# Regrouping the end of the attention layer and moving the load of x_out in a two-layer graph network

## The chip, the cores and the metric

The kernel runs on one core of one Trainium2 chip. The metric is the device time of one execution in microseconds, as the median of several runs.

## The reference, cut to what matters

There are 1250 nodes with 512 features and 40000 edges, sorted by destination. The first layer is graph attention with 8 heads, followed by a feed-forward network with Gelu; the second layer adds up messages along the same edges and runs a batch-normed two-layer network.

```python
# first layer, per edge (source s, destination d), 8 heads of 64 channels
e     = sum_c( leaky_relu(xl[s] + xr[d], 0.2) * att )
alpha = softmax of e over the edges of one destination
x     = x + sum over edges( alpha * xl[s] ) + bias
x     = x + gelu(layernorm(x) @ W1 + b1) @ W2 + b2
x     = layernorm(x_in + x)
# second layer
aggr  = sum over edges( relu(x[s] + edge_attr @ W_e + b_e) )
h     = (1 + eps) * x + aggr
h     = silu(bn(h @ V1 + c1)) @ V2 + c2
out   = layernorm(x + silu(bn(h)))
```

## The kernel before, in words

Nodes are sorted by their number of incoming edges and cut into ten blocks of 128 (one node per partition). Block b has KB[b] edge slots per node: 44, 40, 37, 35, 33, 32, 31, 29, 27, 25. "Row" below means one edge slot of one block: 128 rows of a table, gathered by one indirect DMA that GpSimd (POOL) issues. The first layer has 333 such gathers (tile xg, from the table xl_t), the second layer another 333 (tile xs, from the table xb_t).

**The first layer** (function `attention`) takes the blocks from 9 down to 0. A block is cut into groups of at most 20 rows, and a group into chunks of at most 5 rows (CN). Here G0 and G1 are the groups of block 1 in the kernel before, H0, H1 and H2 those of block 0 (20, 16 and 8 rows). For every chunk, `scores` gathers the rows and runs three long VectorE (DVE) instructions on them (two into z, one into S). After the last chunk of a group, `softmax` takes the running maximum, and ScalarE (ACT) takes the exponential into w. One group later, `weigh` multiplies the rows of each chunk by w: the first `na` rows on ACT, eight instructions a row, the others in one DVE instruction; then TensorE (PE) adds the rows up in PSUM (tile pacc, one buffer, two matmuls a row). Two groups later, `merge` adds pacc to the block's sum on DVE, at chunk 0 of that group. So at every chunk the program issues the scores of one group and the weighing of the group before it; in the last chunk of a group all that is left of that weighing is issued at once.

When a block is merged for the last time, `head_of` normalises it and transposes it (hT), and `body_of` runs its feed-forward network: 16 steps f, each with eight matmuls into pu, a Gelu on ACT into uT and two matmuls into py two steps later. The steps are fed into the other work by calls of `part()`, three to a chunk (the quota). `end_of` adds py, normalises again, and writes the block twice: a plain store to xo_t from the SP queue, and a scatter to xb_t from POOL. Chunks of rows lie in seven buffers (GB); a buffer comes free when PE has added its rows.

The instructions of `attention` on DVE, ACT, PE and POOL go through wrappers (V, A, T, G) that keep the order of the program on their engine. Instructions that are written with `nc.vector` or `nc.scalar`, as in `begin`, `features_of` and `second`, have no such order: the scheduler puts them where it finds room.

**The second layer** (function `second`) first loads all of xo_t into x_out by ten loads of 256 KB from the SP queue. Then it walks the edges in units of 8 (block 9 first): `turn` transposes the edge features on PE and copies them to eaT, `edges` gathers four rows at a time into xs (five buffers), PE computes the edge term pe, and DVE runs two instructions for every pair of rows (`tensor_add`, then a maximum and a sum into pd). `finish` needs x_out of its block after the block's last edge. Features of an edge span are gathered by `features_of`; a span that doesn't start at slot 0 first gets a small DVE instruction (wx, line 1428).

All instructions of the wrappers show line 1059 in the profile; they are told apart by their tiles.

Of the kernel before, what the change touches and what calls it, by code (L numbers as in the profile page):

```python
# [7 lines left out]
F32 = mybir.dt.float32  # L8
BF16 = mybir.dt.bfloat16
I32 = mybir.dt.int32  # L10
AF = mybir.ActivationFunctionType
# [5 lines left out]
P = 128  # L17
# [5 lines left out]
ED = 64  # L23
# [699 lines left out]
def gnn_kernel(ctx, tc, x, src, dst, edge_attr, ln1_g, ln1_b, Wl, Wr, att, gat_bias,  # L723
# [301 lines left out]
    def short_path():  # L1025
        with ExitStack() as sa:
            fast = sa.enter_context(tc.tile_pool(name="fast", bufs=1))
            fdram = sa.enter_context(tc.tile_pool(name="fdram", bufs=1, space=DRAM))
            xb_t = fdram.tile([N + 1, D], F32, name="xb_t")
            xo_t = fdram.tile([NP, D], F32, name="xo_t")  # L1030
            eps1 = row(eps, 1, "eps1", fast)
            nc.vector.tensor_scalar(eps1, eps1, 1.0, None, op0=OP.add)
            back = fast.tile([P, P], F32, name="back")
            nc.vector.tensor_scalar(back, jp, float(-V0), None, op0=OP.is_equal)
            lone = fast.tile([P, 1], F32, name="lone")
            nc.vector.tensor_scalar(lone, jp[:, 0:1], float(-VN), -0.1 * BIG, op0=OP.is_le, op1=OP.mult)
            s2 = sa.enter_context(ExitStack())
            early = {}
            with ExitStack() as s1:
                attention(s1, xb_t, xo_t, back, lone, lambda: begin(s2, early))  # L1040
            second(s2, early, xb_t, xo_t, eps1, back)

    def attention(s1, xb_t, xo_t, back, lone, follow):

# [121 lines left out]
        def body_of(b, y, hT):  # L1166

            py = aq.tile([P, D], F32, name="py", bufs=2)
            nf = FF // P
            uTs = []  # L1170
            for f in range(nf + 2):
                if f < nf:
                    pu = aq.tile([P, P], F32, name="pu", tag="pu", bufs=3)
                    for k in range(KD):
                        T.matmul(pu, w1[:, k, f * P:(f + 1) * P], hT[:, k, :], start=(k == 0), stop=(k == KD - 1))
                    uT = bp.tile([P, P], F32, name="uT", bufs=4)
                    A.activation(uT, pu, AF.Gelu, bias=cols[:, f:f + 1])
                    uTs.append(uT)
                if f == nf:
                    held["hT"] -= 1  # L1180
                if f >= 2:
                    T.matmul(py, uTs[f - 2], w2[:, f - 2, :], start=(f == 2), stop=(f == nf + 1))
                yield
            others.append(end_of(b, y, py))
# [90 lines left out]
        def weigh(g):  # L1275

            w, n = g["w"], g["n"]
            g["gd"] = gd = sp.tile([P, HEADS], F32, name="gd")
            V.tensor_reduce(gd, w[:, :n, :].rearrange("p n h -> p h n"), axis=AX.X, op=OP.add)
            g["pacc"] = aq.tile([P, D], F32, name="pacc")  # L1280
            for c, (c0, cn) in enumerate(g["cuts"]):
                na = (cn + c % 2) // 2
                xv = g["xg"][c][:, na:cn, :].rearrange("p n (h c) -> p n h c", c=CX)[:, :, :, 0:CH]
                V.tensor_mul(xv, xv, w[:, c0 + na:c0 + cn, :, None].to_broadcast([P, cn - na, HEADS, CH]))
                for j in range(c0, c0 + cn):
                    if j < c0 + na:
                        xv = row_of(g, j)
                        for h in range(HEADS):
                            A.activation(xv[:, h, :], xv[:, h, :], AF.Copy, scale=w[:, j, h:h + 1])
                    if g["quota"] > 0:  # L1290
                        g["quota"] -= 1
                        part()
                    add_up(g, j)
                yield
# [50 lines left out]
        over = {}  # L1345
        groups = []
        for b in ORDER:
            cuts = [(0, 20), (20, 16), (36, 8)] if b == 0 else parts(KB[b], GN)
            for k0, n in cuts:
                groups.append(dict(b=b, k0=k0, n=n, first=(k0 == 0), last=(k0 + n == KB[b]), cuts=parts(n, CN), xg=[]))  # L1350
        groups[0]["cuts"] = [(0, 2)] + [(2 + a, k) for a, k in parts(groups[0]["n"] - 2, CN)]
# [4 lines left out]
        for i, g in enumerate(groups):  # L1356
            if g["first"]:
                if i:
                    blk, ahead = ahead, None
                blk["m"] = low  # L1360
                if g["b"] == 0:
                    drain("acc", 1)
                    held["acc"] += 1
                    blk.update(over)
            g["blk"] = blk
            g["S"] = sp.tile([P, GN + 1, HEADS], F32, name="S")
            nc_ = len(g["cuts"])
            for c in range(nc_):
                scores(g, c)
                if c == nc_ - 1:  # L1370
                    softmax(g)
                if c == 0:
                    if g["first"] and g["b"] != ORDER[-1]:
                        ahead = normed_of(g["b"] - 1)
                    if g["last"]:
                        rows_of(blk)
                        if ahead:
                            others.append(xr_of(ahead))
                    if merging:
                        merge(merging)  # L1380
                    weighing = weigh(before) if before else None
                step_others()
                todo = 0
                if weighing:
                    todo = len(before["cuts"]) - c if c == nc_ - 1 else 1
                quota = 3
                for _ in range(todo):
                    before["quota"] = quota
                    next(weighing, 0)
                    quota = before["quota"]  # L1390
                for _ in range(quota):
                    part()
                step_lates()
            merging, before = before, g
# [7 lines left out]
        while going or done or ready or others:  # L1402
            step_others()
            part()
            step_lates()

    def begin(s2, early):

# [21 lines left out]
        gather(ea[:, :en * ED], edge_attr, wx)  # L1430
        return ea

    def second(s2, early, xb_t, xo_t, eps1, back):

        vp = s2.enter_context(tc.tile_pool(name="vp", bufs=1))
        v1, v2, we, ep = (early[k] for k in ("v1", "v2", "we", "ep"))
        x_out = vp.tile([P, NB, D], F32, name="x_out")
        for b in (NB - 1, *range(NB - 1)):
            nc.sync.dma_start(x_out[:, b, :], xo_t[b * P:(b + 1) * P, :])
        hT = vp.tile([P, KD, N], F32, name="hT5")  # L1440
        z1 = vp.tile([P, 2 * KD, N], F32, name="z1")
        st1 = vp.tile([P, 2 * KD, 3, 6], F32, name="st1")
# [18 lines left out]
        with ExitStack() as s3:  # L1461
# [2 lines left out]
            hq = s3.enter_context(tc.tile_pool(name="hq", bufs=1, space=PSUM))  # L1464
            pend = {u: ea for u, ea in zip(spans, early["features"])}

            def turn(b, e0, en, c0, cn):

                at = spans.index((b, e0, en))
                if c0 == 0:  # L1470
                    for u in spans[at:at + 2]:
                        if u not in pend:
                            pend[u] = features_of(ep, *u)
                ea = pend[b, e0, en]
                pt = hq.tile([P, KD, P], F32, name="pt5")
                eaT = ep.tile([P, KD, P], F32, name="eaT")
                for j in range(0, cn, 2):
                    wd = min(2, cn - j) * ED
                    nc.tensor.transpose(pt[:wd, j // 2, :], ea[:, (c0 + j) * ED:(c0 + j) * ED + wd], ident)
                full = cn // 2  # L1480
                if full:
                    nc.scalar.copy(eaT[:, :full, :], pt[:, :full, :])  # L1482
                if cn % 2:
                    nc.scalar.copy(eaT[:ED, full, :], pt[:ED, full, :])
                return eaT

            def edges(b, at0, cn, eaT, pd):
                for d0 in range(0, cn, 4):
                    dn = min(4, cn - d0)
                    xs = xp_.tile([P, 4, D], F32, name="xs")  # L1490
                    for j in range(dn):
                        at = at0 + d0 + j
# [1 line left out]
                    for j in range(0, dn, 2):  # L1494
# [4 lines left out]
                            kk = P if m == 2 else ED  # L1499
                            nc.tensor.matmul(pe[:, i, :], eaT[:kk, q, :], we[:kk, i, :], start=True, stop=True)  # L1500
                        xv = xs[:, j:j + m, :]
                        nc.vector.tensor_add(xv, xv, pe[:, :m, :])  # L1502
                        nc.vector.scalar_tensor_tensor(pd[:, :m, :], xv, 0.0, pd[:, :m, :], op0=OP.max, op1=OP.add)  # L1503
                    yield

            def finish(b, pd):
# [8 lines left out]

            units = [(b, e0, en, c0, min(8, en - c0)) for b, e0, en in spans for c0 in range(0, en, 8)]
            work, at = None, 0
            eaT = turn(*units[0])
            for n, (b, e0, en, c0, cn) in enumerate(units):
                if e0 == 0 and c0 == 0:  # L1520
                    pd = hq.tile([P, 2, D], F32, name="pd")
                    if b == 0:
                        nc.tensor.matmul(pd[:, 0, :], back, h9, start=True, stop=True)
                        nc.vector.memset(pd[:, 1, :], 0.0)
                    else:
                        nc.vector.memset(pd, 0.0)
                ahead = turn(*units[n + 1]) if n + 1 < len(units) else None
                for _ in edges(b, KO[b] + e0 + c0, cn, eaT, pd):
                    if work is not None and next(work, 0) == 0:
                        work = None  # L1530
# [128 lines left out]
```

## Time and profile before

| what | value |
|---|---|
| median of 3 runs | 1665.33 us (1662.75 to 1666.01) |
| profiled execution | 1664.86 us, span 1663.1 us |
| granted TensorE clock, mean | 0.906 |
| PE / DVE / ACT / POOL busy | 1295.3 / 1286.2 / 631.2 / 833.5 us |
| scores of block 1 begin | 754.24 us |
| last pacc matmul ends | 991.5 us |
| last scatter to xb_t issued | 1042.19 us |
| first gather of the second layer | 1048.28 us |
| last gather of the second layer | 1495.5 us |

Times are microseconds from the start of the span. In lines of the timeline the columns are start, duration, engine, line, operation, tiles and shape, count, and in brackets how long the engine was idle before and what it waited for. In the table of stretches the columns are the length, and for each engine the busy time and the number of instructions, then the granted clock, the busy share of the DMA engines and the rate.

### The profile page before, as it was taken

The page shows a single profiled execution, that of the slowest core. Times are in us where ns is not written, and L with a number is a line of the kernel's source. Part 1 is how long each engine was busy: PE and PEld are TensorE (multiplying, and loading weights), DVE is VectorE, ACT ScalarE, POOL GpSimd, SP SyncE. Part 2 cuts the span into 40 slices and gives each one's busy share as a digit, 9 for nine tenths or more (in the row PEclk, how much of TensorE's full clock was granted, in tenths as well). Part 3 has the DMA queues.
Part 4 walks back from the last instruction along what each step waited for, and adds up shares of the span by engine and source line. Part 5 has one row for each costly group of instructions (what it writes and reads, how often), then busy time and mean ns, then how long its engine had stood idle before and what let it go on. Part 6 is the DMA issues. An engine that isn't in the chain of part 4 may idle for free.

```text
span 1663.1 us, 14065 instructions
## 1 busy us (share of the span) xinstructions
PE 1295.3 (78%) x4281; PEld 660.7 (40%) x4281; DVE 1286.2 (77%) x1384; ACT 631.2 (38%) x1900; POOL 833.5 (50%) x762
## 2 busy tenths in 40 slices
PE   5752678888878886869697889587888898889891
PEld 5430225454444443525253446233333343334451
DVE  4918999898888889898999841598999689986123
ACT  0211456666556565657565663000000110001422
POOL 1058755444535465554646410677777757770002
PEclk9975779899989898979899899799989999999995
DMA  4526764343434343544444313777777757770001
GB/s 141 217 68 179 255 210 132 97 118 89 125 93 139 106 135 96 140 108 124 133 118 110 102 49 133 231 227 217 226 223 222 217 165 219 226 208 9 1 1 64
DMA packets 77857, 235.79 MB, mean 142 GB/s; under 512 B 14689, under 2 KB 15167, under 8 KB 77261
## 3 DMA queue, kind: packets, MB, share of 16 engines
q0 software_dynamic: 60160, 200.09, 41.7%
q1 hardware_dynamic: 16205, 32.12, 5.4%
q10 hardware_dynamic: 1408, 2.60, 0.4%
q8 instruction: 36, 0.59, 0.1%
q14 instruction: 48, 0.39, 0.1%
HBM read 216.71 MB, written 18.17 MB: 141 GB/s over the span
## 4 chain that ended last, share of the span: by engine, by line
PE 28%; DVE 16%; issue 16%; ACT 14%; DMA 10%; POOL 5%; SPq 0%; DVEq 0%; POOLq 0%; ACTq 0%
PE pacc L1059 12%; ACT xg L1059 9%; DMA xs<-xb_t,src_i 7%; DVE z L1059 5%; PE pu L1059 5%; PE py L1059 4%; POOL xs L746 3%; DVE pd L1503 3%; PE pe L1500 3%; DVE S L1059 2%; ACT L1059 2%; DMA xg<-xl_t,src_i 2%; PE pm L1059 2%; DVE xs L1502 2%; PE pz L1449 1%
## 5 line engine op out<-in xcount | busy, mean ns | idle before, releaser
L1059 POOL DMA_INDIRECT xg<-xl_t,src_i x333 | 425.6, 1278 | 335.2 <-issue 192.4
L1059 PE MATMUL pacc<-xg,ident 128*128 128x512 f32 x666 | 382.7, 698 | 186.1 <-ACT xg L1059 178.8
L746 POOL DMA_INDIRECT xs<-xb_t,src_i x333 | 317.3, 953 | 117.2 <-issue 78.6
L1500 PE MATMUL pe<-we,eaT 128*128 128x512 f32 x666 | 332.7, 632 | 49.2 <-DVE xs L1502 48.0
L1059 ACT ACTIVATE xg<-xg,w 128x64 f32<-128x64 f32 x1344 | 333.8, 338 | 0.0
L1059 PEld LDWEIGHTS pacc<-xg,ident 128*128 128x128 f32 x666 | 133.7, 216 | 393.7 <-ACT xg L1059 271.8
L1059 DVE TENSOR_TENSOR z<-xg,nxr 128x2600 f32<-128x2600 f32 (+2 forms) x75 | 192.0, 2559 | 67.1 <-DMA xg<-xl_t,src_i 40.4
L1502 DVE TENSOR_TENSOR xs<-xs,pe 128x1024 f32<-128x1024 f32 (+1 forms) x170 | 202.8, 1193 | 38.2 <-DMA xs<-xb_t,src_i 22.9
L1059 PEld LDWEIGHTS pu<-hT,w 128*128 128x128 f32 x1280 | 180.9, 204 | 84.7 <-issue 77.0
L1500 PEld LDWEIGHTS pe<-we,eaT 128*128 128x128 f32 x666 | 121.3, 199 | 225.5 <-DVE xs L1502 111.7
L1503 DVE SCALAR_TENSOR_TENSOR pd<-xs,pd 128x1024 f32<-128x1024 f32 (+1 forms) x170 | 204.4, 1202 | 1.5
L1059 DVE TENSOR_TENSOR z<-z,patt 128x2600 f32<-128x2600 f32 (+2 forms) x75 | 191.9, 2559 | 2.6
L1059 DVE TENSOR_REDUCE S<-z 128x40 f32<-128x2600 f32 (+2 forms) x75 | 191.8, 2558 | 2.6
L1059 PE MATMUL pu<-hT,w 128*128 128x128 f32 x1280 | 183.5, 290 | 4.1 <-ACT hT L1059 4.1
L1059 PE MATMUL py<-w,uT 128*128 128x512 f32 x320 | 169.8, 615 | 1.7 <-ACT uT L1059 1.7
L1059 ACT ACTIVATE uT<-pu,cols 128x128 f32<-128x128 f32 x160 | 58.2, 365 | 130.1 <-PE pu L1059 129.6
L1482 ACT COPY eaT<-pt 128x512 f32<-128x512 f32 (+3 forms) x46 | 24.7, 537 | 208.7 <-PE pe L1500 173.9
L1059 DVE TENSOR_TENSOR xg<-xg,w 128x1024 f32<-128x1024 f32 (+2 forms) x75 | 98.9, 1322 | 0.0
L738 POOL DMA_INDIRECT out_dram<-o,v_i x10 | 9.9, 990 | 146.3 <-DVE o L1620 143.6
L1059 ACT ACT_TABLE_LOAD x63 | 80.8, 1283 | 5.4 <-PE pu L1059 4.3
L1449 PE MATMUL pz<-hT,v 128*128 128x512 f32 (+1 forms) x192 | 72.3, 518 | 5.3 <-ACT z L1457 5.3
L1574 PE MATMUL pz<-z,v 128*128 128x512 f32 (+1 forms) x192 | 70.4, 528 | 5.2 <-ACT z L1565 5.2
(222 smaller groups left out, 914.3 us busy)
## 6 DMA issues: line engine op xcount, KB each, us to landing
w<-in_L_gnn_W_dram SPq DMA_DIRECT2D x8, 1024.0 KB
xg<-xl_t,src_i POOLq DMA_INDIRECT x333, 3.8
xs<-xb_t,src_i POOLq DMA_INDIRECT x333, 3.7
v<-in_L_gnn_W_dram SPq DMA_DIRECT2D x2, 2048.0 KB
xo_t<-xo SPq DMA_DIRECT2D x10, 256.0 KB
x_out<-xo_t SPq DMA_DIRECT2D x10, 256.0 KB
xl_t<-xo ACTq DMA_DIRECT2D x9, 260.0 KB
x_sb<-in_x_dram SPq DMA_DIRECT2D x1, 2304.0 KB
```

What stands on the lines that cost most here:

```text
L738: s = nc.gpsimd.indirect_dma_start(out=table, out_offset=bass.IndirectOffsetOnAxis(ap=idx, axis=0), in_=rows, in_offset=None, bounds_check ...
L746: return nc.gpsimd.indirect_dma_start(out=rows, out_offset=None, in_=table, in_offset=bass.IndirectOffsetOnAxis(ap=idx, axis=0))
L1059: ins = getattr(engine, name)(*args, **kw)
L1449: nc.tensor.matmul(pz[:, :nn], w[:, k, f * P:(f + 1) * P], src_t[:, k, n0:n0 + nn], start=(k == 0), stop=(k == nk - 1))
L1482: nc.scalar.copy(eaT[:, :full, :], pt[:, :full, :])
L1500: nc.tensor.matmul(pe[:, i, :], eaT[:kk, q, :], we[:kk, i, :], start=True, stop=True)
L1502: nc.vector.tensor_add(xv, xv, pe[:, :m, :])
L1503: nc.vector.scalar_tensor_tensor(pd[:, :m, :], xv, 0.0, pd[:, :m, :], op0=OP.max, op1=OP.add)
L1574: nc.tensor.matmul(pzs[i][:, :nn], v2[:, k, f * P:(f + 1) * P], z1[:, k, n0:n0 + nn], start=(k == 0), stop=(k == 2 * KD - 1))
```

## The change: what it does

1. Block 1 is cut into groups of 16, 14 and 10 rows instead of 20 and 20; block 0 into 10, 16, 10 and 8 rows instead of 20, 16 and 8. The projection of the next block (`xr_of`) starts at the second group of a block instead of the last.
2. In the very last group ACT weighs one row of each chunk instead of two.
3. In the body of block 0 an activation with Sqrt on a dummy column follows the last Gelu.
4. The first two copies to eaT and the first memset of pd in the second layer go through the wrappers A and V, and so stand behind the last instructions of the first layer on ACT and DVE.
5. The ten loads of x_out are issued in the first unit of edges, behind the `tensor_add` that ends its second step, and that unit's steps are 2, 4 and 2 rows instead of 4 and 4.

```diff
+                V, A = attention(s1, xb_t, xo_t, back, lone, lambda: begin(s2, early))
+            second(s2, early, xb_t, xo_t, eps1, back, V, A)
...
                 if f == nf:
                     held["hT"] -= 1
+                    if not b:
+                        A.activation(sp.tile([P, 1], F32, name="none_"), ln_eps, AF.Sqrt)
...
-                na = (cn + c % 2) // 2
+                na = 1 if g is groups[-1] else (cn + c % 2) // 2
...
-            cuts = [(0, 20), (20, 16), (36, 8)] if b == 0 else parts(KB[b], GN)
+            cuts = {0: [(0, 10), (10, 16), (26, 10), (36, 8)], 1: [(0, 16), (16, 14), (30, 10)]}.get(b, parts(KB[b], GN))
...
                     if g["last"]:
                         rows_of(blk)
-                        if ahead:
-                            others.append(xr_of(ahead))
+                    if ahead and i and groups[i - 1]["first"]:
+                        others.append(xr_of(ahead))
...
         x_out = vp.tile([P, NB, D], F32, name="x_out")
-        for b in (NB - 1, *range(NB - 1)):
-            nc.sync.dma_start(x_out[:, b, :], xo_t[b * P:(b + 1) * P, :])
...
-            def turn(b, e0, en, c0, cn):
+            def turn(b, e0, en, c0, cn, act=nc.scalar):
...
-                    nc.scalar.copy(eaT[:, :full, :], pt[:, :full, :])
+                    act.copy(eaT[:, :full, :], pt[:, :full, :])
...
-                for d0 in range(0, cn, 4):
-                    dn = min(4, cn - d0)
+                for d0, dn in [(0, 2), (2, 4), (6, 2)] if at0 == KO[NB - 1] else [
+                        (d, min(4, cn - d)) for d in range(0, cn, 4)]:
...
-                        nc.vector.tensor_add(xv, xv, pe[:, :m, :])
+                        add = nc.vector.tensor_add(xv, xv, pe[:, :m, :])
...
+                    if at0 == KO[NB - 1] and d0 == 2:
+                        for k in (NB - 1, *range(NB - 1)):
+                            after(nc.sync.dma_start(x_out[:, k, :], xo_t[k * P:(k + 1) * P, :]), [add],
+                                  "behind the first gathers")
...
-            eaT = turn(*units[0])
+            eaT = turn(*units[0], A)
...
-                        nc.vector.memset(pd, 0.0)
-                ahead = turn(*units[n + 1]) if n + 1 < len(units) else None
+                        (nc.vector if n else V).memset(pd, 0.0)
+                ahead = turn(*units[n + 1], nc.scalar if n else A) if n + 1 < len(units) else None
```

More of the change, by code (lines that the diff above doesn't have):

```diff
@@ L1039, in short_path @@
             with ExitStack() as s1:
-                attention(s1, xb_t, xo_t, back, lone, lambda: begin(s2, early))
-            second(s2, early, xb_t, xo_t, eps1, back)
+                V, A = attention(s1, xb_t, xo_t, back, lone, lambda: begin(s2, early))
+            second(s2, early, xb_t, xo_t, eps1, back, V, A)
     def attention(s1, xb_t, xo_t, back, lone, follow):
@@ L1405, in attention @@
             step_lates()
+        return V, A
     def begin(s2, early):
@@ L1431, in features_of, with second @@
         return ea
-    def second(s2, early, xb_t, xo_t, eps1, back):
+    def second(s2, early, xb_t, xo_t, eps1, back, V, A):
         vp = s2.enter_context(tc.tile_pool(name="vp", bufs=1))
@@ L1481, in turn @@
                 if full:
-                    nc.scalar.copy(eaT[:, :full, :], pt[:, :full, :])
+                    act.copy(eaT[:, :full, :], pt[:, :full, :])
                 if cn % 2:
-                    nc.scalar.copy(eaT[:ED, full, :], pt[:ED, full, :])
+                    act.copy(eaT[:ED, full, :], pt[:ED, full, :])
                 return eaT
             def edges(b, at0, cn, eaT, pd):
-                for d0 in range(0, cn, 4):
-                    dn = min(4, cn - d0)
+                for d0, dn in [(0, 2), (2, 4), (6, 2)] if at0 == KO[NB - 1] else [
+                        (d, min(4, cn - d)) for d in range(0, cn, 4)]:
                     xs = xp_.tile([P, 4, D], F32, name="xs")
```

## The prediction

> **What bounds the kernel now.** I read, in this order, the table of stretches around the layers' seam, the timelines of DVE, ACT, PE and POOL there, and the waits of the second layer. First the stretches.
>
> ```profile
> core 0: us, PE busy (x) PEld busy (x) DVE busy (x) ACT busy (x) POOL busy (x), PEclk, DMA share, GB/s
> 848.00:895.00 47.00, 44.57 (x184) 25.83 (x183) 41.83 (x23) 29.13 (x99) 27.80 (x22) 1.00 0.44 121
> 895.00:938.00 43.00, 27.56 (x59) 11.72 (x60) 41.23 (x41) 27.05 (x94) 21.91 (x16) 0.83 0.37 99
> 938.00:964.00 26.00, 25.68 (x105) 15.35 (x103) 19.20 (x19) 16.88 (x52) 6.11 (x5) 0.96 0.25 80
> 964.00:992.00 28.00, 23.90 (x67) 11.54 (x67) 9.35 (x18) 22.91 (x86) 0.20 (x1) 0.94 0.00 1
> 1005.00:1035.00 30.00, 28.19 (x160) 20.00 (x158) 2.70 (x8) 9.23 (x20) 1.02 (x1) 1.00 0.26 97
> 1042.20:1048.30 6.10, 0.00 (x0) 0.00 (x0) 0.00 (x0) 0.00 (x0) 1.01 (x2) 0.80 0.88 303
> ```
>
> Until 964 DVE is nearly full, except where a body runs and PE is full. Then scores are over, and ACT and PE carry the end; from 1005 PE alone does the body of block 0; in the last 6.1 us every engine waits for DMA. Next DVE and ACT.
>
> ```profile
> 953.60 0.69 DVE L1059 TENSOR_TENSOR oacc<-oacc,pacc 128x512 f32<-128x512 f32 x1 [6.52 <-PE pacc L1059]
> 983.70 0.69 DVE L1059 TENSOR_TENSOR oacc<-oacc,pacc 128x512 f32<-128x512 f32 x1 [15.30 <-PE pacc L1059]
> 1007.28 0.15 DVE L1428 TENSOR_SCALAR wx<-w_i 128x1 int32<-128x1 int32 x1 [11.37 <-DMA ea<-in_edge_attr_dram,wx]
> 1034.94 0.69 DVE L1059 TENSOR_TENSOR xx<-xx,py 128x512 f32<-128x512 f32 x1 [22.53 <-PE py L1059]
> 1036.57 0.91 DVE L1526 MEMSET pd<- 128x1024 f32 x1 [0.21 <-issue]
> ```
>
> ```profile
> 973.03 15.38 ACT L1059 ACTIVATE xg<-xg,w 128x64 f32<-128x64 f32 x64
> ...
> 1036.42 0.59 ACT L1482 COPY eaT<-pt 128x512 f32<-128x512 f32 x1 [3.63 <-DVE st L1059]
> 1037.75 0.59 ACT L1482 COPY eaT<-pt 128x512 f32<-128x512 f32 x1 [0.75 <-PE pt L1479]
> 1038.36 1.28 ACT L1059 ACT_TABLE_LOAD   x1
> ```
>
> DVE waits in the merges for pacc; pacc waits for ACT, whose last eight rows take 15.38 us (1.92 a row; mostly 2.0). Between the last py and the scatter, a memset, two copies and a table load of the second layer stand in the way. Then POOL:
>
> ```profile
> 1042.19 1.01 POOL L1059 DMA_INDIRECT xb_t<-xb,v_i  x1 [28.48 <-DVE xb L1059]
> 1048.28 0.99 POOL L746 DMA_INDIRECT xs<-xb_t,src_i  x1 [5.09 <-DMA x_out<-xo_t]
> ```
>
> ```profile
> POOL xs L746 <- issue: 78.6, 258, 0.3
> POOL xs L746 <- DVE pd L1503: 15.8, 16, 5.7
> ```
>
> From 1048.28 to the last gather at 1495.5 POOL issues 349 gathers (333 rows, 16 edge spans) every 1.257 us, 438.7 us of 447.2. So the second layer starts with POOL's first gather and shifts with it one for one. The sum is made against this execution's 1664.86 us (span 1663.1 and 1.8 around it), 0.5 under the median 1665.33.
>
> **The change, step by step.** *1. Scores up to the last softmax (964.0 now).* Two more groups each cost DVE a softmax (0.91: 936.86 to 937.77), a sum gd (0.3) and a middle merge (0.96 from 946.12, and 0.61 from 953.60): 2.8 each; shorter reductions give back some 0.5 in all: +5.1. Block 1 has nine chunks for eight: a chunk of five rows takes 8.58 and one of four 6.95, so 0.43 a chunk is fixed: +0.4. Weighing done before that softmax: H0 and one chunk of H1 now (10+2 rows on DVE); then 5+8+3, +4 rows at 0.57 (1.14 for two): +2.3. DVE work: **+7.8**.
>
> DVE's waits from 754 to 964 sum to 17.0 now: gathers 4.7 in G0 and 4.8 in H0 (buffers that PE frees late), pacc 0.9, 6.5, small rest. With 16, 14, 10, 10, 16, 10, 8 rows the live chunks fall and H0's gather waits go. But a short group after a long one bunches the rest of the weighing. The price is in the trace: after the softmax that ends at 964.03, six ACT rows and three body steps take until 983.7, 19.6 us; with five rows 17.6, with three 13.6 (2.0 less each). DVE's own work until it needs pacc: muls 2.8, a chunk 8.6, sums 1.0 = 12.4 for block 1's middle group, so 5.2 waiting; 1.1+7.0+1.7 = 9.8 for its last, 3.8; 3.4+7.0+1.0 = 11.4 for block 0's group of 16, 8.2. With G0's 4.7, 21.9 against 17.0: **+4.9** (bounds: −5 if the merges wait half as long and G0's waits go too; +16 if each of the three exponentials is also late by 3.8 us, as the one at 941.54 is, whose softmax ended at 937.77). Last softmax: 964.0+7.8+4.9 = 976.7.
>
> *2. From there to the last pacc: 27.5 us now* (964.03 to 991.53; ten ACT rows). Then five ACT rows, three of them on the path: exponential 0.3, 3 × 2.0, a table load and a Gelu among them 1.56 (966.34 to 967.90), three rows on PE 2.7 = 10.6. Merge 0.7. The single pacc buffer holds up the last group until then: gd 0.2, a three-row mul on DVE 1.75, seven rows on PE at 0.86 = 6.0: 8.0. Sum 19.3: **−8.2**. Last pacc at 996.0, +4.5.
>
> *3. To the start of block 0's body: 1004.73 now*, behind the last four steps of block 1's body. A body needs 18 part() calls. Block 1's starts in chunk 2 of the group of 16, both times; chunks left after that: four now (12 calls, six left over for the end), six then (18). So the body of block 0 starts when hT is ready: 999.55 − 991.53 = 8.0 after pacc, less the table load and Gelu that now stand before h (1.16: h would follow at 995.34, not 996.50) = 6.9. 996.0+6.9 = 1002.9: **−1.8**.
>
> *4. The body: 30.2 now*, of which one stall at 1009.3 (1.7) is block 1's norm and goes. But PE then enters after idling through the head. The row: after 2.3 us of idling, pu at 997.85 took 1.69 for eight matmuls and py 1.91 for two at 999.33, against 1.05 and 1.02 when warm, until about 1002: 2.0 lost. So **+0.3**. The Trainium skill (TensorE: Matmul & The Clock Gate, Part 1: The HAM clock gate) states that PE falls to half clock after an idle window of about 3.4 us and needs as long to recover; that speaks against this step. By the rule the loss would be 1.7 instead of the row's 2.0. The row shows it after a shorter idle time.
>
> *5. Last py to the scatter: 7.25 now* (1034.94 to 1042.19). Without memset, copies and load, by the same steps elsewhere: add, statistics, sqrt, reciprocal, product 1007.35 to 1009.54 = 2.19, then xo, xb, scatter 1040.18 to 1042.19 = 2.01: 4.2, **−3.05**. The Sqrt table load (1.28) is hidden behind the 2.6 us of last py matmuls after the last Gelu; uncovered it costs 1.28. The copies and the memset move behind xo and xb; cover: the scatter's flight.
>
> *6. Scatter to first gather: 6.09 now*, while ten loads of x_out (2.6 MB) fill the DMA engines (share 0.88). The ten scatters of the output land 2.8 us (median) after issue with little else under way. Bounds 2.8 and 6.1; I take 3.3, nearest to the free ones, with a little for the store to xo_t that still runs beside it: **−2.8**. SP then waits for a DVE add; nothing but those loads is queued on SP. They now slow gathers some 11 us later: free, since xs holds 16 to 20 rows (20 us of POOL) and a gather lands within 6.2 us at the worst; block 9's finish needs x_out only at its 25th row. If not covered, up to 2.5.
>
> *7. The second layer* keeps its 447.2 us; its POOL stalls (12 us from 1335 to 1368, after a wx on DVE waited 9.66) may fall otherwise when the scheduler places things anew: 0, ±4.
>
> Sum: +12.7 −8.2 −6.3 (block 1's leftover steps and the shorter head: 13.2 to 6.9) +0.3 −3.05 −2.8 = −7.35: 1657.5 against 1664.86, as a median 1658.0.
>
> **Rivals.** *A, slower: the single pacc buffer.* Each merge of a short group starts a new wait, the next group's exponential comes late behind it, and so on. Price: 3.8 more at each of three merges, 11.4: 1669.4. For it: ACT's exponential at 941.54. Against it: two-chunk groups leave two chunks without any weighing in the group of 16, where the lag is worked off. It decides from the point where the last softmax lies 20 us later than now (12.7 + 7.35); beyond 23.4 the kernel is slower.
>
> *B, more gain: the lag vanishes.* Fewer live chunks mean no waits for gathers (4.7), and half the merge waits (8.6 less): 13.3 more, cut to 10 by PE, which is full while bodies run: 1648.0. For it: DVE's gather waits all lie where PE frees buffers late. Against it: PE has 0.86 a row and 1.75 a step to do in any order.
>
> *C, no change: wx takes DVE.* The third wx on line 1428 waits for a gather of edge features that landed 15.75 us after the last pacc (1007.28 − 991.53), beside 4 MB of weights. Now it blocks DVE while PE is busy anyway. If the scheduler puts it before the reciprocal of block 1's norm, xo of block 1, and behind it on ACT the second Gelu of block 0's body, wait until 996.0+15.75 = 1011.7 instead of 1005.4: +6.3, 1664.3.
>
> *D, the move of x_out does nothing,* because the gather waits for its scatter alone and that isn't slowed: 2.8 back, 1660.8; a part of my own case.
>
> **How the numbers follow.** My case (with D) 0.39, B 0.20, C 0.16, A 0.25. A measurement here tells 0.2% (3.3 us) from no change. Mine and B are faster, 0.59; C is the same, 0.16; A slower, 0.25. My own range is 1652 to 1662 (D, and 2 to 6 us for step 7 and the merge waits). To leave out 2 in 10 the whole range goes from 1646 (B with step 7's luck) to 1671 (A with 1 or 2 us of it).
>
> **What would show it.** Right: last softmax near 977, merge waits near 5, 4 and 8 us, last pacc within 20 us of it, body of block 0 at 1003 without block 1's steps behind pacc, 4.2 us from py to the scatter, the first gather near 1041 and the last near 1488. Wrong: a last softmax past 984 (A), one before 970 (B), a wx wait on DVE between the last pacc and xo of block 1 (C), or 6 us again between scatter and gather (D).

## The result: no change that a measurement can tell

The kernel after takes 1665.31 us (median of 20 executions, 1658.73 to 1669.41), the kernel before on the same chip 1663.39 (20 executions, 1659.54 to 1671.71). The ratio is 1.0004 [0.999, 1.0018]: +0.7 us, between −1.7 and +3.0; the medians, 1.9 apart, lie within that. The profiled execution has a span of 1665.4 us (before 1663.1) at a granted clock of 0.907 (0.906).

The forecast's likeliest case, −7.4 us, did not come: 1665.31 lies outside the range of that case, 1652 to 1662, and only inside the whole one, 1646 to 1671. All later steps came nearly as worked out; the first, the time up to the last softmax, grew by nearly half as much again as forecast (18.4 for 12.7, below) and took the rest back.

The profiles differ by some microseconds before they even reach the change: block 2's last softmax, behind which the scores of block 1 begin, starts at 751.85 in before and at 754.77 in after, and between 748.4 and 764.4 in the kernels further below. So each stage is counted from its own beginning.

| stage, from instruction to instruction | before | after | forecast | measured |
|---|---|---|---|---|
| block 2's last softmax to the last softmax | 211.45 | 227.98 | +12.7 | +16.5 |
| to the read of the last pacc | 28.33 | 20.35 | −8.2 | −8.0 |
| to the first matmuls of block 0's body | 13.10 | 6.22 | −6.3 | −6.9 |
| to the add of the last py | 30.21 | 30.82 | +0.3 | +0.6 |
| to the scatter | 7.25 | 4.20 | −3.05 | −3.05 |
| to the first gather | 6.09 | 3.73 | −2.8 | −2.4 |
| to the last gather | 447.2 | 448.8 | 0 | +1.6 |
| sum | | | −7.35 | −1.6 |

The first row varies from profile to profile. Four profiles with the old groups (before, e1, e6, e7) give 208.9 to 212.8, mean 210.6; four with the new ones (after, e2, e8, e12) give 227.9 to 231.6, mean 229.0: **+18.4**. With that the sum is +0.3, and the measurement says +0.7.

### The profile page after: what moved, and what is told of

The parts are those of the page before. It is cut to its first block, busy times and chain, and to the rows that moved or that the text cites. A ratio compares the mean times of both kernels' runs of the same rounds, so it can differ in the third digit from the quotient of the medians.

```text
span 1665.4 us, 14076 instructions
## 1 busy us (share of the span) xinstructions
PE 1296.3 (78%) x4281; PEld 658.6 (40%) x4281; DVE 1291.7 (78%) x1406; ACT 631.6 (38%) x1890; POOL 826.0 (50%) x762
## 4 chain that ended last, share of the span: by engine, by line
PE 28%; DVE 17%; issue 16%; ACT 14%; DMA 8%; POOL 5%; DVEq 0%; POOLq 0%; ACTq 0%
PE pacc L1059 13%; ACT xg L1059 8%; DMA xs<-xb_t,src_i 6%; DVE pd L1504 5%; PE pu L1059 5%; DVE z L1059 4%; PE py L1059 4%; POOL xs L746 3%; PE pe L1501 3%; ACT L1059 2%; DVE S L1059 2%; DVE xs L1503 2%; PE pm L1059 2%; DMA xg<-xl_t,src_i 1%; PE pz L1450 1%
## 5 line engine op out<-in xcount | busy, mean ns | idle before, releaser
L1059 POOL DMA_INDIRECT xg<-xl_t,src_i x333 | 417.7, 1254 | 350.9 <-issue 184.9
L1059 PE MATMUL pacc<-xg,ident 128*128 128x512 f32 x666 | 377.7, 691 | 191.1 <-ACT xg L1059 186.7
L1059 ACT ACTIVATE xg<-xg,w 128x64 f32<-128x64 f32 x1328 | 329.7, 338 | 0.0
L1503 DVE TENSOR_TENSOR xs<-xs,pe 128x1024 f32<-128x1024 f32 (+1 forms) x170 | 202.4, 1191 | 33.5 <-DMA xs<-xb_t,src_i 20.6
L1059 PEld LDWEIGHTS pu<-hT,w 128*128 128x128 f32 x1280 | 176.5, 200 | 80.9 <-issue 72.6
L1059 PE MATMUL pu<-hT,w 128*128 128x128 f32 x1280 | 179.4, 286 | 4.7 <-ACT hT L1059 4.7
```

The lines of the kernel that those rows point to most:

```text
L1059: ins = getattr(engine, name)(*args, **kw)
L1503: add = nc.vector.tensor_add(xv, xv, pe[:, :m, :])
```

## The profile after

The table of stretches, cut where after has its own stages (columns as for before):

```profile
core 0: us, PE busy (x) PEld busy (x) DVE busy (x) ACT busy (x) POOL busy (x), PEclk, DMA share, GB/s
851.00:898.00 47.00, 40.97 (x159) 22.55 (x158) 37.64 (x29) 32.49 (x111) 32.53 (x27) 1.00 0.56 160
...
943.00:983.00 40.00, 35.19 (x127) 19.46 (x127) 32.51 (x29) 27.10 (x94) 6.86 (x5) 0.92 0.14 41
983.00:1003.10 20.10, 15.58 (x38) 5.93 (x36) 8.16 (x19) 12.73 (x44) 0.00 (x0) 1.00 0.00 0
...
1044.30:1048.10 3.80, 3.80 (x14) 1.84 (x12) 0.89 (x1) 0.58 (x1) 1.05 (x2) 1.00 0.34 129
```

In the first stretch DVE has lost four microseconds of work (37.64 of 47; 41.83 before): it now waits there. In the second, as long as the scores last, it is idle for 7.5 of 40. The third is the shortened end. In the last line the DMA share is 0.34 where it was 0.88, and the stretch is 3.8 long instead of 6.1. DVE's timeline in after:

```profile
768.25 2.32 DVE L1059 TENSOR_TENSOR z<-xg,nxr 128x2080 f32<-128x2080 f32 x1 [2.00 <-DMA xg<-xl_t,src_i]
...
779.74 2.33 DVE L1059 TENSOR_TENSOR z<-xg,nxr 128x2080 f32<-128x2080 f32 x1 [3.33 <-DMA xg<-xl_t,src_i]
...
789.64 2.33 DVE L1059 TENSOR_TENSOR z<-xg,nxr 128x2080 f32<-128x2080 f32 x1 [1.20 <-DMA xg<-xl_t,src_i]
...
799.92 2.33 DVE L1059 TENSOR_TENSOR z<-xg,nxr 128x2080 f32<-128x2080 f32 x1 [1.08 <-DMA xg<-xl_t,src_i]
...
879.04 0.69 DVE L1059 TENSOR_TENSOR acc<-acc,pacc 128x512 f32<-128x512 f32 x1 [8.87 <-PE pacc L1059]
...
902.47 0.69 DVE L1059 TENSOR_TENSOR t<-pacc,rd 128x512 f32<-128x512 f32 x1 [1.63 <-PE pacc L1059]
...
973.21 0.69 DVE L1059 TENSOR_TENSOR oacc<-oacc,pacc 128x512 f32<-128x512 f32 x1 [7.08 <-PE pacc L1059]
...
994.20 0.69 DVE L1059 TENSOR_TENSOR oacc<-oacc,pacc 128x512 f32<-128x512 f32 x1 [8.61 <-PE pacc L1059]
...
1018.67 0.15 DVE L1431 TENSOR_SCALAR wx<-w_i 128x1 int32<-128x1 int32 x1 [7.79 <-DMA ea<-in_edge_attr_dram,wx]
...
1044.27 0.91 DVE L1059 MEMSET pd<- 128x1024 f32 x1 [0.21 <-issue]
```

The first four lines are waits for gathered rows at the start of block 1; they are taken up at the end. The 15.30 before block 0's last middle merge (983.70 in before) has become 8.61, but three waits for pacc ahead of it are 8.87, 1.63 and 7.08 where before had 0.92 and 6.52. Of wx it is told below. The memset stands at 1044.27, behind xb. What comes ahead of the wait of 8.87 is seen on ACT in after:

```profile
853.48 0.58 ACT L1059 COPY acc<-pacc 128x512 f32<-128x512 f32 x1 [2.93 <-PE pacc L1059]
...
861.46 0.37 ACT L1059 ACTIVATE uT<-pu,cols 128x128 f32<-128x128 f32 x1 [2.24 <-PE pu L1059]
861.84 1.28 ACT L1059 ACT_TABLE_LOAD   x1
863.13 0.28 ACT L1059 ACTIVATE w<-S 128x88 f32<-128x88 f32 x1
...
1038.00 1.28 ACT L1059 ACT_TABLE_LOAD   x1
1039.30 0.20 ACT L1059 ACTIVATE none__5844<-ln_eps 128x1 f32<-128x1 f32 x1
...
1043.24 0.56 ACT L1059 COPY eaT<-pt 128x512 f32<-128x512 f32 x1
```

The softmax of the middle group begins on DVE at 856.33 and its sums are written at 857.2; its exponential `w<-S` runs at 863.13, 5.9 later. ACT was at the copy of the preceding group's pacc (it waited 2.93 for it), at rows and at Gelus of the body, one of which waits 2.24 for PE. From the exponential to the merge it is then 15.9. That this lag makes the wait is my reading; e9 below tests a part of it. The last three lines are the seam: the table load stands directly behind the last Gelu, and the first copy to eaT behind xo. POOL's timeline and its waits in the second layer (time in all, times, longest) in after:

```profile
1044.34 1.01 POOL L1059 DMA_INDIRECT xb_t<-xb,v_i  x1 [23.60 <-DVE xb L1059]
1048.07 0.99 POOL L746 DMA_INDIRECT xs<-xb_t,src_i  x1 [2.71 <-PE pt L1480]
```

```profile
POOL xs L746 <- DVE pd L1504: 17.4, 16, 7.0
```

The longest stall of the second layer is 7.0 for 5.7. On PE, in after, block 0's body starts so, after four transposes and 4.62 of idling ahead of them; the granted clock is 0.50 from 1009.3 to 1014.6 and 1.00 after that:

```profile
1009.32 5.44 PE L1059 MATMUL pu<-hT,w 128*128 128x128 f32 x24 [0.55 <-ACT hT L1059]
```

## Experiments

Theory T: the seam (parts 3 to 5 of the change) brings its 5 us, and the new groups with the new last rows (1 and 2) cost about as much. The rivals are told with the runs. Edits are shown against after unless another kernel is named. e1 to e4 shared one chip and 35 executions of before, e5 to e8 another and 17, e9 to e12 a third and 35.

**e1: the seam alone**, groups and weighing as before.

```diff
-                na = 1 if g is groups[-1] else (cn + c % 2) // 2
+                na = (cn + c % 2) // 2
...
-            cuts = {0: [(0, 10), (10, 16), (26, 10), (36, 8)], 1: [(0, 16), (16, 14), (30, 10)]}.get(b, parts(KB[b], GN))
+            cuts = [(0, 20), (20, 16), (36, 8)] if b == 0 else parts(KB[b], GN)
...
-                    if ahead and i and groups[i - 1]["first"]:
-                        others.append(xr_of(ahead))
+                        if ahead:
+                            others.append(xr_of(ahead))
```

> Parts 3, 4 and 5 alone (Sqrt ahead of time, order of the first copies and memset, x_out behind the first gathers); groups, na and xr_of as before. Theory T, the groups take back what the seam brings: after the last py the scatter follows in 4.2 us and the first gather 3.7 us after that, against 7.25 and 6.09; so 5.4 us less than before, some 1658, and the last gather 5.4 us earlier too. Rival R, the seam's gain is lost later: the first gather comes 5.4 us earlier, but POOL's stalls near 1330 grow by as much and the time stays at 1663 to 1664.

Measured: 1662.07 against 1668.02, 0.9973 [0.9955, 0.9991], −4.5 us. In its profile last softmax to first gather takes 79.5 us (before 85.0), and the second layer 447.2 as before. POOL's timeline in e1:

```profile
1033.62 1.01 POOL L1059 DMA_INDIRECT xb_t<-xb,v_i  x1 [25.43 <-DVE xb L1059]
1037.35 0.99 POOL L746 DMA_INDIRECT xs<-xb_t,src_i  x1 [2.72 <-PE pe L1501]
...
1324.47 0.95 POOL L746 DMA_INDIRECT xs<-xb_t,src_i  x1 [5.65 <-DVE pd L1504]
```

The seam is worth what steps 5 and 6 said of it. The rival R, that a stall of the second layer gives it back, falls: the stall is 5.65, before had 5.67.

**e2: groups and last rows alone**, the seam as before (the reverse of e1: `cuts`, `xr_of` and `na` of after in the kernel before).

> Parts 1 and 2 alone (groups, xr_of, one ACT row in the last group); the seam as before. T: last softmax 16 to 17 us later, 8 us back to the last pacc, 7 us back to the start of block 0's body, body 0.6 longer: 2 to 3 us slower than before, 1666. R: the groups are a wash and nothing else counts: as before, 1663 to 1664.

Measured: 1671.73, 1.0024 [1.0005, 1.0044], +4.0 us. The last softmax comes 228.6 after block 2's last, 17.1 later than in before; pacc 20.34 and 37.05 to the last py follow as in after. POOL in e2:

```profile
1041.66 1.01 POOL L1059 DMA_INDIRECT xb_t<-xb,v_i  x1 [26.31 <-DVE xb L1059]
1047.39 0.99 POOL L746 DMA_INDIRECT xs<-xb_t,src_i  x1 [4.72 <-DMA x_out<-xo_t]
```

With x_out loaded at once the first gather comes 5.73 after the scatter. The groups cost 4.0, the seam brings 4.5: together about nothing, as after shows. T stands.

**e3 and e4: the groups of one block each.** In e3 block 1 keeps its old groups, in e4 block 0 does. Seam, weighing and `xr_of` are after's.

```diff
-            cuts = {0: [(0, 10), (10, 16), (26, 10), (36, 8)], 1: [(0, 16), (16, 14), (30, 10)]}.get(b, parts(KB[b], GN))
+            cuts = {0: [(0, 10), (10, 16), (26, 10), (36, 8)]}.get(b, parts(KB[b], GN))
```

```diff
-            cuts = {0: [(0, 10), (10, 16), (26, 10), (36, 8)], 1: [(0, 16), (16, 14), (30, 10)]}.get(b, parts(KB[b], GN))
+            cuts = {0: [(0, 20), (20, 16), (36, 8)], 1: [(0, 16), (16, 14), (30, 10)]}.get(b, parts(KB[b], GN))
```

> The changed kernel with block 1 cut into 20 and 20 as before; block 0 stays at 10, 16, 10, 8. T: the extra group of block 1 costs DVE 3.2 us and a merge wait of 8.9 us, of which some comes back at the next merge, since now three chunks of block 1 are weighed in one step; the 18 steps of block 1's body still fit in. So 4 to 10 us less than the changed kernel: 1655 to 1661. R: as the changed kernel, 1665.

> The changed kernel with block 0 cut into 20, 16, 8 as before; block 1 stays at 16, 14, 10. T: block 1's cuts cost some 8 us until the last softmax, and the six leftover steps of block 1's body are back behind the last pacc; the two ACT rows less in the last group save 4, the seam 5.4: 1660 to 1664. If the cuts of block 1 bring the gain instead: under 1657. R: 1665.

Measured: e3 1663.89, 0.9983 [0.9966, 1.0]; e4 1669.57, 1.0019 [1.0002, 1.0037]. The time to the last softmax grows by 11.9 and by 8.9 over the mean of the old groups: both blocks pay, and the sum, 20.8, is a little over the 18.4 of both together. Only block 0's groups are paid back: from the last softmax to the last pacc e3 takes 20.6, e4 28.6, as long as before, although e4's last group has one ACT row a chunk. My expectation of e4 was a miss: the shorter end on which it rested did not come. By the ratios e3 is 3.5 us under after, a little less than the 4 to 10 that T expected, and the two intervals overlap.

e3 also shows something that after does not. DVE, then PE, in e3:

```profile
1000.93 0.18 DVE L1059 BATCH_NORM_AGGREGATE mv<-st 128x2 f32<-128x6 f32 x1
1011.05 0.15 DVE L1431 TENSOR_SCALAR wx<-w_i 128x1 int32<-128x1 int32 x1 [9.94 <-DMA ea<-in_edge_attr_dram,wx]
1011.13 0.15 DVE L1059 RECIPROCAL rs<-rs 128x1 f32<-128x1 f32 x1
```

```profile
1012.63 1.13 PE L1059 MATMUL py<-w,uT 128*128 128x512 f32 x2 [3.52 <-ACT uT L1059]
```

This is rival C: wx waits 9.94 for a gather, block 1's reciprocal stands behind it, xo behind that on ACT, the Gelus behind xo, and PE stalls 3.52 in block 0's body. From pacc to the last py e3 takes 39.49, after 37.04.

**e5: two pacc buffers** (the room comes from py's second buffer). Theory P: the single pacc buffer makes the merge waits.

```diff
-            py = aq.tile([P, D], F32, name="py", bufs=2)
+            py = aq.tile([P, D], F32, name="py", bufs=1)
...
-            g["pacc"] = aq.tile([P, D], F32, name="pacc")
+            g["pacc"] = aq.tile([P, D], F32, name="pacc", bufs=2)
```

> The changed kernel with two pacc buffers (py gets one instead of two). P, the single pacc buffer makes the merge waits: the waits of 8.9, 7.1 and 8.6 us on pacc fall by half or more and the kernel is 8 to 12 us faster than the changed one, 1653 to 1658. Q, the rows that are left of a long group are weighed in one step, in order on ACT (2 us a row) and PE, whatever the buffers: the waits stay within 2 us of what they were, at most the last rows start 1 to 2 us earlier, and the time stays within 3 us of the changed kernel, or rises by what one py buffer costs.

Measured: 1673.86 against 1667.92, 1.0045 [1.0025, 1.0065]. DVE in e5:

```profile
889.62 0.69 DVE L1059 TENSOR_TENSOR acc<-acc,pacc 128x512 f32<-128x512 f32 x1 [9.06 <-PE pacc L1059]
...
984.87 0.69 DVE L1059 TENSOR_TENSOR oacc<-oacc,pacc 128x512 f32<-128x512 f32 x1 [7.53 <-PE pacc L1059]
```

The waits are 9.06, 7.53 and, at 1005.86, 8.61; after had 8.87, 7.08 and 8.61. P falls. What the kernel loses lies ahead of block 1: in its profile block 2's last softmax starts at 764.4, 9.6 later than in after, and the stages behind it take about as long as there. The lost py buffer is the only other edit; which wait it makes was not followed up.

**e6: the seam, and wx computed at once.** Theory W: the wx that waits 9.66 (before) or 9.67 (e1) in the second layer is what makes POOL stall there. e6 is e1 with all wx computed where the layer begins.

```diff
+        wxs["t"] = er.tile([P, len(spans)], I32, name="wxs")
+        for i, (b, e0, en) in enumerate(spans):
+            if e0:
+                nc.vector.tensor_scalar(wxs["t"][:, i:i + 1], w_i[:, b:b + 1], float(e0), None, op0=OP.add)
...
-            wx = ep.tile([P, 1], I32, name="wx")
-            nc.vector.tensor_scalar(wx, w_i[:, b:b + 1], float(e0), None, op0=OP.add)
+            at = spans.index((b, e0, en))
+            wx = wxs["t"][:, at:at + 1]
```

> The seam parts alone with the old groups, and all eight wx columns computed at once where the first features are fetched, so that no wx stands on DVE behind a gather of features later. W: the wait of 10 us on DVE at about 1310 makes POOL's stalls of 12 us after 1324; without it both go and the kernel is 5 to 11 us faster than the seam alone, 1651 to 1657. V: the stalls come from the dense work that starts there (PE and ACT); they stay and the time is that of the seam alone, 1658 to 1662.

Measured: 1651.2 (6 executions), 0.9909 [0.9874, 0.9943], −15.2 us: the lowest ratio of all versions. From the first to the last gather it takes 441.7 where e1 takes 447.2 (and e7 below, on e6's chip, 448.7). DVE in e1, which has no counterpart in e6, then POOL in e6 where e1 stalled 5.65:

```profile
1306.37 0.15 DVE L1431 TENSOR_SCALAR wx<-w_i 128x1 int32<-128x1 int32 x1 [9.67 <-DMA ea<-in_edge_attr_dram,wx]
```

```profile
1325.66 0.95 POOL L746 DMA_INDIRECT xs<-xb_t,src_i  x1 [2.04 <-DVE pd L1509]
```

W stands: POOL's waits for DVE's pd fall from 17.2 in e1 to 10.6 in all. The profiles account for 5.4 of the seam, 5.5 of the second layer and 0.9 between the last softmax and the last py, 12 in all; the interval, −21 to −9.5, holds that.

**e7: e1 without the early Sqrt.** In the prediction the table load of 1.28 is hidden by that activation.

```diff
-                    if not b:
-                        A.activation(sp.tile([P, 1], F32, name="none_"), ln_eps, AF.Sqrt)
```

> The seam parts without the early Sqrt. From the add of the last py to the scatter: 4.2 us with it; mine is 5.5 without (the table load of 1.28 uncovered). If the order of the copies and of the memset brought nothing by itself: 7.2. One run, 1.3 us more than the seam alone, which a single time can't tell.

Measured (one execution): 1664.57; the last py to the scatter takes 1039.37 to 1043.58 = 4.21, with the activation 4.20. ACT in e7:

```profile
1037.24 1.28 ACT L1059 ACT_TABLE_LOAD   x1
1041.04 0.29 ACT L1059 ACTIVATE rs<-mv,ln_eps 128x1 f32<-128x1 f32 x1 [2.52 <-DVE mv L1059]
```

The load runs as soon as ACT comes to it, while the activation that needs it still waits for mv. The dummy is worth nothing, and my 5.5 was a miss; what had held the load up in before was the copy to eaT ahead of it.

**e8: after with two ACT rows a chunk in the last group** (`na` as before).

> The changed kernel with the old shares of ACT in the last group (two rows of four in each chunk, na as before). From the last softmax to the read of the last pacc: 20.35 us in the changed kernel. If ACT's rows set that end, 4 us more; if the DVE multiplications and PE's rows behind the middle merge set it, 0 to 1 us more.

Measured (one execution): 1668.05; from the last softmax to the last pacc's read 19.38, with one row 20.35. One row was meant to shorten the end; it lengthens it by 0.97. Of the two expected cases, 4 us more and 0 to 1 us more, neither came; the second is the nearer. DVE in e8:

```profile
997.15 0.69 DVE L1059 TENSOR_TENSOR oacc<-oacc,pacc 128x512 f32<-128x512 f32 x1 [8.62 <-PE pacc L1059]
...
997.93 2.35 DVE L1059 TENSOR_TENSOR xg<-xg,w 128x1024 f32<-128x1024 f32 x2
```

In after that product is 3.42 for 2.35. DVE's share of the last rows stands behind the merge's wait, so every row given to DVE there is on the path, while the wait itself (8.62 against 8.61) does not shrink.

**e9: after with fewer ACT rows in long groups.** If ACT's rows are what holds the merges up, DVE should take rows of the chunks that a shorter group follows.

```diff
+                follower = groups[g["i"] + 1:g["i"] + 2]
+                if g["b"] < 2 and follower and len(g["cuts"]) > len(follower[0]["cuts"]) <= c + 1:
+                    na = 1
...
+        for i, g in enumerate(groups):
+            g["i"] = i
```

> The changed kernel; in the chunks that are weighed together because the next group has fewer chunks (the last two of 16 and of 14 rows in block 1, the last three of 16 in block 0) ACT takes one row instead of two or three, eight rows less, and DVE eight more (4.6 us). Q1, ACT's rows set the merge waits: those of 8.9 and 7.1 us fall by 4 us or more each, the last softmax comes 4 to 7 us earlier, 1658 to 1661. Q2, PE's rows and steps set them: the waits fall by what DVE works more, the last softmax stays where it was or comes up to 2 us later, 1664 to 1667.

On the chip of e9 to e12 before took 1763.14, some 5.7% longer than on the others. The profiles of these four show it in the second layer, 529 to 549 us from the first to the last gather; so of them only the ratios and the stages of the first layer are used.

Measured: 0.9962 [0.9932, 0.9992]; after was 1.0004 on its chip. DVE in e9:

```profile
875.11 0.69 DVE L1059 TENSOR_TENSOR acc<-acc,pacc 128x512 f32<-128x512 f32 x1 [4.11 <-PE pacc L1059]
...
968.80 0.69 DVE L1059 TENSOR_TENSOR oacc<-oacc,pacc 128x512 f32<-128x512 f32 x1 [4.27 <-PE pacc L1059]
```

The waits fall by 4.8 and 2.8, but DVE works longer for it: the products of the first chunk take 4.48 for 2.88. Softmax to merge falls from 22.71 to 19.47 and from 19.77 to 18.56, and the last softmax comes 2.8 earlier. The result lies between Q1 and Q2: ACT's rows are part of the wait, not all of it; the exponential is still 3.9 late (860.47, after sums that were ready at 856.6).

**e10, e11, e12: which groups to keep once wx is out of the way.** e10 is e3, e11 is e6 with e9's rule, e12 is after, each with e6's wx.

> e3_block0 with all wx computed at once. There the third wx stood in front of the reciprocal of block 1's norm and DVE waited 9.94 us for it. C: from the last pacc to the add of the last py 37.1 us as in the changed kernel, not 39.5; together with the 5.6 us that the later wx cost in the second layer 8 us less than e3_block0, 1656. If PE had lost nothing by it: 39.5 stays, 1658.

> e6_seam_wx with one ACT row instead of two in the last three chunks of block 0's group of 16. Q1: after the last softmax seven ACT rows instead of ten; 3 to 4 us earlier at the last pacc, and at most that at the end, since PE then still has block 1's leftover steps: 1648 to 1650. Q2: unchanged, 1651.

> The changed kernel with all wx computed at once. T: the groups cost 4 us against the seam alone, with the wx out of the way as with it: 5.6 to 10 us less than the changed kernel and 4 us more than e6_seam_wx, 1655. If the groups had lost by wx alone: as e6_seam_wx, 1651.

Measured: 0.9937 [0.9908, 0.9966], 0.9943 [0.9913, 0.9972] and 0.999 [0.9963, 1.0018]. With wx gone e10 takes 36.52 from pacc to the last py where e3 took 39.49: 3.0 us is rival C's price here. e11's rule shortens the last softmax to the last py from 70.70 (e6) to 67.65. To the last pacc's read e11 takes 27.46 for 28.89, less than the 3 to 4 us that Q1 expected there. And e12 is slower by about 0.5%, some 9 us here, than e10, from which it differs in block 1's groups alone; e11, with the old groups and e9's rule, is level with e10. So the part of the change that loses is block 1's groups. My expectation of e12 was a miss: 0.14% under after is not told from nothing, where 5.6 to 10 us were expected. So on this chip, with its longer second layer, W's gain is not borne out for the changed kernel, and its size there stays open. So does whether e10 or e11 beats e6: they ran on different chips, and the intervals overlap.

## Why the prediction's range held, and where its sum was wrong

The time fell into the whole range by its width, which was made for the rivals, and not by the mechanism that I thought likeliest; that is luck. Of the four signs named for being wrong none came (the last softmax started at 982.75, short of 984), so they were set too wide.

**Step 1 failed: the waits before the last softmax, +4.9.** The DVE work was right: +18.4 less the waits' growth of 10.9 leaves +7.5, forecast +7.8, and DVE's busy time in the stretch goes from 191.7 in before to 199.1 in after. The waits themselves, summed from the brackets of DVE's timeline between block 2's last softmax and the last of all, mean of the same four profiles each:

| DVE waits for | old groups | new groups | change | forecast |
|---|---|---|---|---|
| gathered rows (ahead of z) | 8.8 | 7.7 | −1.1 | −4.8 |
| pacc | 7.1 | 19.1 | +12.0 | +9.8 |

Two terms were mis-sized, by about as much. One is the gathers, 3.7 over: I let the waits of H0 vanish and kept G0's at 4.7. DVE in before, G0 and then H0:

```profile
766.51 2.87 DVE L1059 TENSOR_TENSOR z<-xg,nxr 128x2600 f32<-128x2600 f32 x1 [1.55 <-DMA xg<-xl_t,src_i]
...
778.20 2.87 DVE L1059 TENSOR_TENSOR z<-xg,nxr 128x2600 f32<-128x2600 f32 x1 [1.90 <-DMA xg<-xl_t,src_i]
...
789.79 2.87 DVE L1059 TENSOR_TENSOR z<-xg,nxr 128x2600 f32<-128x2600 f32 x1 [1.27 <-DMA xg<-xl_t,src_i]
...
862.09 2.87 DVE L1059 TENSOR_TENSOR z<-xg,nxr 128x2600 f32<-128x2600 f32 x1 [1.62 <-DMA xg<-xl_t,src_i]
...
873.73 2.87 DVE L1059 TENSOR_TENSOR z<-xg,nxr 128x2600 f32<-128x2600 f32 x1 [1.85 <-DMA xg<-xl_t,src_i]
...
885.37 2.87 DVE L1059 TENSOR_TENSOR z<-xg,nxr 128x2600 f32<-128x2600 f32 x1 [1.32 <-issue]
```

H0's did vanish in after, but those at the start of block 1 grew to 7.6 (2.00, 3.33 and 1.20 in the group of 16, 1.08 at the first chunk of the next). They go with block 1's cuts: 8.3 in e4, which has the new ones, 5.5 in e3, which has the old. That chunks of four rows are used up faster than buffers for the next rows come free is the likely reason; no run tried it, so the cause stays open.

The other is the merge of block 1's middle group, 8.87 for 5.2 (8.4 to 9.4 in the four). From the end of the softmax to it 21.9 us pass where I had 17.6, and the exponential came 5.9 late, the lag that rival A priced at 3.8 and that I had put into the upper bound. The other two merges were 1.63 and 7.08 for 3.8 and 8.2, so that pacc is only 2.2 over in all. That the lag is the cause is argued; e9, which shortened it to 3.9 together with ACT's rows, cut the wait to 4.11.

**Step 2** was right in size (−8.0), wrong in part of its reason: the shorter next-to-last group does it (e4 without it: 28.6); the row that ACT gives up costs up to 1 us (e8).

**Steps 3 and 4** together: −6.3 for −6.0. The body starts behind hT without steps of block 1. PE's slow start cost in after more than the row said: the 24 pu took 5.44 at a granted clock of 0.50, where before's took 2.84 at 1.00, a loss of 2.6 for 2.0, after 4.62 of idling. In the eight profiles with block 0's new groups the 24 pu take 4.40 to 5.49, so 2.0 is not far off; but the row's own terms (0.64, 0.89 and 0.23) add up to 1.8. By the rule of the Trainium skill (TensorE: Matmul & The Clock Gate, Part 1: The HAM clock gate), about 3.4 us of sustained work until the clock is full again, I had estimated 1.7; here the half clock lasted longer, 5.3 us. The stall of 1.7 in block 1's norm went as forecast.

**Step 5** was exact in size (−3.05). Its term for the table load was not a hiding at all (e7): the order of the copies alone does it.

**Step 6**: −2.4 for −2.8, so **rival D** is refuted. The first gather came 3.73 after the scatter where I had 3.3. The ten loads were issued later, from 1059.4 on, and no issue on POOL waited more than 0.31 from the first gather until 1328.

**Step 7**: +1.6 for 0 ± 4. The wx that I named there as a chance of the schedule is worth 5.5 us of the second layer when removed (e6); I saw its wait and asked only whether it would shift.

**Rival A** decides when the last softmax lies 20 later; 18.4 came. Its lag was real at one of three merges, its named cause, the single buffer, was not (e5). **Rival B** lost: the waits grew. **Rival C** named the class that came, within 0.2%, but by luck, not by its mechanism. In after wx stood behind block 1's reciprocal (1010.52) and delayed only its xb; e3 shows C at work, at 3.0 us for the 6.3 of its price.

## What to carry to other kernels

Cutting the last groups of a pipeline smaller moves work from its end to its middle: price both from the same rows, and look whether a wait that vanishes in one group turns up in another. A small instruction that the scheduler may place freely and that waits on a DMA can hold a whole engine for ten microseconds; look for it in the brackets of the timeline and compute it early, ahead of any work on the balance of engines. And measure parts apart: here a gain of 4.5 us and a loss of 4.0 lay inside a change that measured as nothing.

## What the runs showed of the hardware

- A table load on ACT (1.28 us) runs when ACT reaches it, not when its activation's operand is ready: with and without a dummy activation ahead, 4.20 and 4.21 us (e1, e7).
- A gather that depends on a scatter came 3.73 us after it with little beside it, 5.73 to 6.09 with ten loads of 256 KB in flight (e1 and after; e2 and before).
- One DVE instruction of 0.15 us that waited on a gather for 9.67 us was followed by a stall of 5.65 on POOL that ended 18 us later (e1); without it the longest stall was 2.15 (e6).
- One chip ran the second layer of four kernels (e9 to e12) in 529 to 549 us from the first to the last gather, where the others took 442 to 449, with the first layer's stages as elsewhere. Why is open, and before was not profiled there.
- After PE had idled for 3.76 to 5.17 us, 24 small matmuls took 4.40 to 5.49 us for 2.84 (eight profiles), and the granted clock was 0.50 meanwhile (after). It was 0.50 too, from 999.3 to 1001, after 2.3 us of idling in before.
